# Turning convolved rows on VectorE instead of TensorE in a window-attention and depthwise-convolution kernel

## The chip, the cores and the metric

The kernel runs on one core of a Trainium2 chip. The core has five engines with queues of their own: TensorE (PE in the profile, its weight loads PEld), VectorE (DVE), ScalarE (ACT), GpSimd (POOL) and SyncE (SP), and 16 DMA engines that move data. The metric is device time in microseconds (us); less is better.

## The reference

Sixteen images of 56 x 56 positions with 384 channels, all float32, go through two layers, each added to its input:

```
x = x + window_attention(group_norm(x))     # shifted by 3, windows 7 x 7, 12 heads of 32
x = x + depthwise_conv3x3(group_norm(x))    # one 3x3 filter per channel, clipped to -1..1, then its sign
```

The group norm has 32 groups of 12 channels and no weights of its own. The second one needs the whole image of the first layer's result before its mean and variance are known, so the convolution of an image can start only when its attention is over.

## The kernel before

*Strips and units.* An image is 8 strips of 7 rows, one row of windows each. A strip (392 positions) is held channels by positions, in 3 chunks of 128 channels. Half a strip, 4 windows, is a unit: 256 units in all, 16 an image. `all_units` walks them. In each unit the heavy work is written in 6 steps (`heavy`): queries, keys (`query_key`, L464) and values (`value`, L477) of the next strip, the scores of the next unit (`scores`, L518), this unit's sums over the exponentials (`add_up`, L589), weighting (`attend`, L609) and, in second halves, the projection (`project`, L648). Around them DVE adds the bias (`softmax`, L535), ACT takes the exponential (`exponential`, L553) and the inverse of the sums (`invert`, L627 and L628, then L629 and L630 on DVE). There is one score buffer in PSUM, which the scores of the next unit may overwrite only after L629 has read the sums.

*Values by key.* `turn` transposes values in squares of 32 on DVE (L488), and `by_key` moves them to their places by 16 DMAs a strip on SP's queue, in pieces of 128 bytes (L500). Input strips are read by POOL's queue in 128-byte pieces (L411) and turned by DVE in squares of 32 (`turn_halves`, L428).

*Light work.* Functions with a time in units are put into a list by `at(when, f, ...)`; in each unit, after each of the 6 steps, those whose time has come are written out in order of time. The order of the program on each engine and on each queue is thus set by these times; an engine and a queue work strictly in that order.

*Convolution.* `project` writes the first layer's result, channels by positions, to DRAM (`mids`). `plan_conv` works on the previous image beside the attention of the current one. The image is cut into 4 bands of BR = 14 rows, times 3 chunks. For each band and chunk, every 1.3 units (0.95 for image 14): `band` loads 14 rows and their neighbours on SP's queue (L696); `pad` writes the normalised rows into a padded buffer (ACT, L711; one border row cleared by POOL where the band is at an edge); `middle` starts the sum with the centre tap and the residual (ACT, L723); eight `tap`s add the other taps on DVE (L736), each a multiply-add over 128 x 784 elements that reads and writes the same sum. When the 3 chunks of a band are done, `store` turns the sums on PE (L747: seven tiles of 112 positions, 3 transposes each, into one PSUM bank), ACT copies the bank out (L748), and SP's queue writes rows of 1,536 bytes, two tiles a DMA (L752).

*The last image* has nothing to hide behind. `plan_last` lays it out after the last unit: `norm_late` (the norm by matmuls, without DRAM), then per band chunks 0 and 1 as above on DVE, and chunk 2 on PE (`convolve`, L773 and L780: the taps as matmuls with diagonal weights, which also turn the sums; `carry` copies and stores, L788 and L791). The bands are loaded one after the other into two buffers of `bpool`. At the very end a check that numbers stayed in range decides on a slower second pass (not taken here).

Of the kernel before, what the change touches and what calls it, by code (L numbers as in the profile page):

```python
# [15 lines left out]
WIN = 7  # L16
# [18 lines left out]
def kernel(  # L35
# [27 lines left out]
    BR = 14  # L63
    NB = H // BR
    R = W + SHIFT
# [6 lines left out]
    LG = 2  # L72
# [9 lines left out]
    io = ctx.enter_context(tc.tile_pool(name="io", bufs=3))  # L82
# [3 lines left out]
    bpool = ctx.enter_context(tc.tile_pool(name="xb", bufs=2))  # L86
    opool = ctx.enter_context(tc.tile_pool(name="o", bufs=5))
# [37 lines left out]

    spare = [
# [11 lines left out]
    def clear_more():  # L138
        nc.gpsimd.memset(power, -0.5)
        nc.gpsimd.memset(ones, 1.0)  # L140
        nc.gpsimd.memset(least, LEAST)
        nc.gpsimd.memset(seen, 0.0)
        for t in (qk[:, :, ST:], *hps):
            nc.gpsimd.memset(t, 0.0)

    def clear_again():
        for t in spare:
            nc.vector.memset(t, 0.0)
# [22 lines left out]
    def load_depthwise():  # L171
        wl = [io.tile([P, LG, C], F32, tag="io", name=f"dwl{n}")[:9, 0, :] for n in range(3)]
        nc.scalar.dma_start(wl[0], w_dw.rearrange("a b c o -> (a b) (c o)"))
        for c in range(NC):
            nc.scalar.dma_start(bo_sb[:, c : c + 1], b_out[c * P : (c + 1) * P].unsqueeze(1))

        nc.vector.tensor_scalar(wl[1], wl[0], -1.0, 1.0, ALU.max, ALU.min)
        nc.vector.tensor_scalar(wl[0], wl[1], 0.0, None, ALU.is_gt)
        nc.vector.tensor_scalar(wl[2], wl[1], 0.0, None, ALU.is_lt)
        nc.vector.tensor_tensor(wl[0], wl[0], wl[2], ALU.subtract)  # L180
        nc.vector.tensor_tensor(wl[0], wl[0], wl[1], ALU.subtract)
        nc.vector.tensor_tensor(wl[0], wl[0], wl[1], ALU.add)  # L182
        pw = bank("pdw")
        for c in range(NC):
            nc.tensor.transpose(pw[:, c * 9 : (c + 1) * 9], wl[0][:, c * P : (c + 1) * P], ident[:9, :9])
        nc.vector.tensor_copy(dw_t, pw[:, : NC * 9].rearrange("p (c t) -> p c t", c=NC))
# [106 lines left out]
    def fetch_late():  # L293

        pairs = group_blocks(C, GS)
        gm = xpool.tile([P, NC, ST], F32, tag="x", name="gm").rearrange("p c n -> p (c n)")[:, : len(pairs) * P]
        gm = gm.rearrange("p (n q) -> p n q", q=P)
        nc.sync.dma_start(gm, gmat)
        dg = xpool.tile([P, NC, ST], F32, tag="x", name="dg").rearrange("p c n -> p (c n)")[:, : 9 * P]
        dg = dg.rearrange("p (t q) -> p t q", q=P)  # L300
        hp = xpool.tile([P, NC, ST], F32, tag="x", name="hp_late").rearrange("p c n -> p (c n)")
        hp = hp[:, : (BR + 2) * (W + 2)].rearrange("p (h w) -> p h w", w=W + 2)
        acc = xpool.tile([P, NC, ST], F32, tag="x", name="acc_late").rearrange("p c n -> p (c n)")
        acc = acc[:, : BR * (W + 2)].rearrange("p (h w) -> p h w", w=W + 2)
        for t in (hp, acc):
            nc.gpsimd.memset(t, 0.0)
        late_tiles.update(gm=gm, dg=dg, hp=hp, acc=acc)
# [382 lines left out]
    def band(b, k, c):  # L690

        lo, hi = max(k * BR - 1, 0), min((k + 1) * BR + 1, H)
        at = lo - (k * BR - 1)
        xb = bpool.tile([P, BR + 2, R], F32, tag="xb", name=f"xb_{b}_{k}_{c}")
        rows = xb[:, at : at + hi - lo, :]
        nc.sync.dma_start(rows, mids[b][:, c, lo:hi, :])  # L696
        bands[b, k, c] = (xb, rows, at, hi - lo)
# [3 lines left out]
    def pad(b, k, c, late=False):  # L701

        coef, cen = coefs[1, b], centers[b]
        xb, rows, at, n = bands.pop((b, k, c))
        hp = late_tiles["hp"] if late else hps[count[0] % 2]
        count[0] += not late
        if k == 0:
            nc.gpsimd.memset(hp[:, 0, :], 0.0)
        if k == NB - 1:
            nc.gpsimd.memset(hp[:, BR + 1, :], 0.0)  # L710
        nc.scalar.activation(  # L711
            hp[:, at : at + n, 1 : W + 1],
            rows[:, :, 0:W],
            AF.Identity,
            bias=coef[:, c, 1:2],
            scale=coef[:, c, 0:1],
        )
        padded[b, k, c] = (hp, xb)

    def middle(b, k, c, late=False):  # L720
        hp, xb = padded[b, k, c]
        acc = late_tiles["acc"] if late else opool.tile([P, BR, W], F32, tag="o", name=f"o_{b}_{k}_{c}")
        nc.scalar.activation(  # L723
            acc[:, :, :W],
            xb[:, 1 : BR + 1, 0:W],
            AF.Identity,
            bias=centers[b][:, c, 1:2],
            scale=centers[b][:, c, 0:1],
        )
        outs[b, k, c] = acc  # L730

    def tap(b, k, c, t):
        dy, dx = divmod(t, 3)
        acc = outs[b, k, c]
        hp, _ = padded[b, k, c]
        nc.vector.scalar_tensor_tensor(  # L736
            acc, hp[:, dy : dy + BR, dx : dx + W], dw_t[:, c, t : t + 1], acc, ALU.mult, ALU.add
        )

    def store(b, k, g, chunks=NC):  # L740
        todo = range(g * LG, min((g + 1) * LG, BR * W // OT))
        flat = [outs[b, k, c].rearrange("p h w -> p (h w)") for c in range(chunks)]
        xo = io.tile([P, LG, C], F32, tag="io", name=f"xo_{b}_{k}_{g}")
        for n, t in enumerate(todo):
            po = bank(f"px_{b}_{k}_{t}")
            for c in range(chunks):
                nc.tensor.transpose(po[:OT, c * P : (c + 1) * P], flat[c][:, t * OT : (t + 1) * OT], ident)  # L747
            nc.scalar.copy(xo[:OT, n, : chunks * P], po[:OT, : chunks * P])  # L748
        n = len(todo)
        first = k * BR * W + g * LG * OT  # L750
        rows = out[b].rearrange("h w c -> (h w) c")[first : first + n * OT, : chunks * P]
        nc.sync.dma_start(rows.rearrange("(t p) c -> p t c", p=OT), xo[:OT, :n, : chunks * P])  # L752
# [3 lines left out]
    def convolve(b, k, c):  # L756
# [5 lines left out]
        tiles = BR * W // OT  # L762
# [19 lines left out]
    def carry(b, k, c):  # L782

        by_token = xpool.tile([P, NC, ST], F32, tag="x", name=f"xc_{k}").rearrange("p c n -> p (c n)")
        tiles = BR * W // OT
# [3 lines left out]
        rows = out[b].rearrange("h w c -> (h w) c")[k * BR * W : (k + 1) * BR * W, c * P : (c + 1) * P]  # L789
# [5 lines left out]

    def plan_last(b, first):

        at(first, norm_late, b)
        at(first + 0.1, center, b, nc.vector)
        for k in range(NB):  # L800
            for c in (2, 0, 1):
                n = 2 * k + c
                when = first + 0.5 + (2 * k if c == 2 else n)
                at(when - (0.1 if c == 2 else 0.2), band, b, k, c)
                at(when - (0.05 if c == 2 else 0.15), pad, b, k, c, c == 2)
                at(when - (0.04 if c == 2 else 0.14), middle, b, k, c, c == 2)
                if c == 2:
                    at(when + 0.2, convolve, b, k, c)
                    at(when + 1.3, carry, b, k, c)
                    continue  # L810
                for i, t in enumerate((0, 1, 2, 3, 5, 6, 7, 8)):
                    at(when + i / 8, tap, b, k, c, t)
            for g in range(-(-BR * W // OT // LG)):
                at(first + 0.5 + 2 * k + 2.02 + 0.01 * g, store, b, k, g, NC - 1)
# [7 lines left out]
    def plan_conv(p, first, step, lead, late, queue):  # L822
# [5 lines left out]
        for n in range(NB * NC):  # L828
            k, c = divmod(n, NC)
            when = first + step * n  # L830
            at(when - 1.3 * step, band, p, k, c)
            at(when - 0.65 * step, pad, p, k, c)
            at(when - 0.45 * step, middle, p, k, c)
            for i, t in enumerate((0, 1, 2, 3, 5, 6, 7, 8)):
                at(when + step * i / 8, tap, p, k, c, t)
            if c == NC - 1:
                tiles = -(-BR * W // OT // LG)
                for g in range(tiles):
                    at(when + step + late + 0.3 * g, store, p, k, g)
# [18 lines left out]
    def heavy(u):  # L858
# [13 lines left out]
        if more:  # L872
            todo[1 if half else 2 * NC - 1].append((by_key, (s + 1, half)))
# [8 lines left out]
    def plan(last_queue):  # L882
        for b in range(1, B):
            plan_load(b)
            plan_conv(b - 1, NU * b, 1.3 if b < B - 1 else 0.95, 3, 0.6, nc.gpsimd)
        at(B * NU - 6, fetch_late)
        for t in range(9):
            at(B * NU - 5 + 0.3 * t, diagonal, t)

    def all_units(fast):  # L890
# [42 lines left out]
        plan_last(B - 1, B * NU)  # L933
# [112 lines left out]
```

## Time and profile before

| | |
|---|---|
| device time, median of 3 runs | 4287.52 us (4286.94 to 4291.69) |
| device time of the profiled execution | 4289.45 us |
| its span | 4287.3 us |
| granted TensorE clock, mean over the span | 0.989 |
| DMA engines, mean share busy, 1000 to 1250 us | 0.49 |
| first and last exponential (L553) | 83.9 and 4148.4 us |
| last projection on PE (L648) | 4161.2 us |
| first tap of the last image | 4174.1 us |

The span starts at the first instruction of the profiled execution. "Busy" is the time in which an engine had an instruction running; for PE it is pipelined, so a busy PE need not be at its peak. In a line of a group, the numbers after the bar are busy time in all and the mean duration of one instruction in ns, then the idle time of the engine just before these instructions and what ended it. In a line of a stretch the figures are PE, PEld, DVE, ACT and POOL busy (with the number of instructions), the granted clock, the DMA engines' share and GB/s. In a line of order in time they are start, duration, engine, line, operation, output <- inputs. In a line of a DMA queue they are packets, MB, and the share of 16 engines' time in that stretch.

### The profile page before, as it was taken

How to read it: one execution, taken by the hardware profiler on the slowest of the kernel's cores; microseconds unless marked ns; L12 is line 12 of the kernel's file. 1: busy time of each engine (PE TensorE's matmuls, PEld its weight loads, DVE VectorE, ACT ScalarE, POOL GpSimd, SP SyncE). 2: the span in 40 equal slices, each digit the busy share in tenths (PEclk: the TensorE clock that was granted, in tenths of full speed). 3: DMA queues.
4: the chain of work that ended last, by engine and by line, in shares of the span. 5: the costliest groups of instructions: out<-in, count | busy, mean ns of one | idle time of the engine just before them, and what ended most of it. 6: DMA issues, size and time to landing. Idle time of an engine off the chain costs nothing. (4 is left out here: it accounts for less than half of the span.)

```text
span 4287.3 us, 156586 instructions
## 1 busy us (share of the span) xinstructions
PE 4182.8 (98%) x68545; PEld 2688.1 (63%) x68545; DVE 3448.4 (80%) x4367; ACT 2482.8 (58%) x5286; POOL 1796.1 (42%) x3160
## 2 busy tenths in 40 slices
PE   5999999999999999999999999999999999999986
PEld 3666666666666666666666666666666666666656
DVE  4556888788887888878888897888889788887875
ACT  2545656566565656656565665656656565665542
POOL 4453545354443544535345443535445344451000
PEclk8999999999999999999999999999999999999988
DMA  4434445454444545445454444545544454543432
GB/s 90 80 66 82 105 106 123 103 109 108 110 100 106 120 99 116 107 100 121 96 114 111 107 103 106 117 106 110 109 107 105 105 122 99 114 105 80 105 97 86
DMA packets 1000294, 445.33 MB, mean 104 GB/s; under 512 B 876922, under 2 KB 938203, under 8 KB 999602
## 3 DMA queue, kind: packets, MB, share of 16 engines
q1 hardware_dynamic: 909776, 273.72, 30.7%
q0 software_dynamic: 87648, 159.12, 15.3%
q8 instruction: 542, 8.88, 0.9%
q10 hardware_dynamic: 2178, 2.38, 0.2%
q14 instruction: 150, 1.23, 0.1%
HBM read 175.31 MB, written 158.46 MB: 78 GB/s over the span
## 5 line engine op out<-in xcount | busy, mean ns | idle before, releaser
L464 PE MATMUL pq<-xn,wq_t 128*128 128x392 f32 x4608 | 1590.5, 496 | 0.4 <-ACT ot L619 0.2
L736 DVE SCALAR_TENSOR_TENSOR o<-hp,dw_t,o 128x784 f32<-128x784 f32 x1504 | 1527.5, 1020 | 49.1 <-ACT o L723 35.8
L411 POOL DMA_DIRECT2D xl<-in_x_dram x1980 | 1328.7, 725 | 179.6 <-DVE xt L428 105.4
L464 PEld LDWEIGHTS pq<-xn,wq_t 128*128 128x128 f32 x4608 | 844.1, 188 | 587.0 <-issue 1.6
L648 PE MATMUL py<-ot,wo_t 128*128 128x392 f32 x2304 | 817.9, 497 | 1.6 <-DVE ot L637 1.6
L477 PE MATMUL pv<-xn,wq_t 128*128 128x392 f32 x2304 | 817.9, 496 | 1.2 <-ACT xn L453 1.2
L471 ACT COPY qk<-pq 128x392 f32<-128x392 f32 x768 | 371.4, 484 | 700.8 <-PE pq L464 697.4
L629 DVE SCALAR_TENSOR_TENSOR ln<-ps,inv 128x588 f32<-128x588 f32 x256 | 197.1, 770 | 538.2 <-ACT inv L628 538.2
L668 POOL COPY y<-y 128x63 f32<-128x63 f32 x128 | 34.1, 267 | 1389.1 <-DVE y L656 1389.0
L477 PEld LDWEIGHTS pv<-xn,wq_t 128*128 128x128 f32 x2304 | 420.8, 189 | 284.9 <-ACT xn L453 2.4
L648 PEld LDWEIGHTS py<-ot,wo_t 128*128 128x128 f32 x2304 | 420.6, 190 | 271.8 <-DVE ot L637 1.9
L484 ACT COPY vt<-pv 128x392 f32<-128x392 f32 x384 | 189.1, 493 | 449.1 <-PE pv L477 448.1
L553 ACT ACTIVATE e<-e 128x1176 f32<-128x1176 f32 x256 | 303.1, 1184 | 236.3 <-DVE e L535 236.3
L518 PEld LDWEIGHTS ps<-qk 32*64 32x64 f32 x24576 | 309.4, 131 | 146.6 <-issue 109.2
L609 PE MATMUL po<-e,v 49*32 49x49 f32 x24576 | 364.0, 212 | 8.1 <-DMA v<-vq 7.8
L535 DVE SCALAR_TENSOR_TENSOR e<-ps,bias 128x1176 f32<-128x1176 f32 x256 | 349.2, 1364 | 25.9 <-PE ps L518 24.7
L609 PEld LDWEIGHTS po<-e,v 49*32 49x32 f32 x24576 | 354.6, 105 | 14.2 <-issue 8.3
L518 PE MATMUL ps<-qk 32*64 32x49 f32 x24576 | 342.1, 226 | 3.5 <-DVE ln L629 2.6
L440 ACT COPY x<-xt 128x196 f32<-128x196 f32 x720 | 225.8, 369 | 93.4 <-DVE xt L428 92.2
L488 DVE STREAM_TRANSPOSE vq<-vt 128x512 f32<-128x512 f32 x384 | 267.6, 698 | 6.7 <-ACT vt L484 6.5
L656 DVE TENSOR_TENSOR y<-py,x 128x392 f32<-128x392 f32 x384 | 215.1, 560 | 62.7 <-PE py L648 57.5
L453 ACT ACTIVATE xn<-x,coef 128x392 f32<-128x392 f32 x384 | 247.2, 713 | 13.9 <-DVE dwl L182 13.9
(152 smaller groups left out, 3722.8 us busy)
## 6 DMA issues: line engine op xcount, KB each, us to landing
v<-vq SPq DMA_DIRECT2D x2048, 48.0 KB
mid<-y POOLq DMA_DIRECT2D x112, 619.5 KB
xl<-in_x_dram POOLq DMA_DIRECT2D x1260, 52.5 KB
out_dram<-xo SPq DMA_DIRECT2D x180, 336.0 KB
xb<-mid SPq DMA_DIRECT2D x96, 472.0 KB
xb<-mid SPq DMA_DIRECT2D x96, 442.5 KB
out_dram<-xo SPq DMA_DIRECT2D x60, 168.0 KB
mid<-y POOLq DMA_DIRECT2D x15, 354.0 KB
```

The costliest lines, as they stand in the source:

```text
L411: nc.gpsimd.dma_start(xz[i * D + lo : i * D + hi, c, k : k + n, :], flat[token : token + n * (hi - lo)].rearrange("(k t) c -> t k c", k=n) ...
L453: nc.scalar.activation(xn[:, c, :, :T], xs[s][:, c, :].rearrange("p (w t) -> p w t", t=T), AF.Identity, bias=coef[:, c, 1:2], scale=coef[: ...
L464: nc.tensor.matmul(pq[:, :ST].rearrange("p (w t) -> p w t", t=T), wq_t[:, c, m * P : (m + 1) * P], xn[:, c, :, :T], start=(c == 0), stop=( ...
L471: nc.scalar.copy(qk[:, m, :ST], pq[:, :ST])
L477: nc.tensor.matmul(pv[:, :ST].rearrange("p (w t) -> p w t", t=T), wq_t[:, c, 2 * C + m * P : 2 * C + (m + 1) * P], xn[:, c, :, :T], start= ...
L488: nc.vector.transpose(vq[:, :, :, m].rearrange("p h n d -> p n h d"), vt[:, m].rearrange("p (n w) (j b) -> p n (w j) b", w=2, b=D),)
L518: nc.tensor.matmul(pp[row * HT : (row + 1) * HT, i, k0 : k0 + T], qk[part, NC * fast + j, q0 : q0 + HT], qk[part, NC * (not fast) + j, q0 ...
L535: nc.vector.scalar_tensor_tensor(e, pp[:, :, : NC * 2 * T].rearrange("q i (n k) -> q i n k", k=T), QSCALE, bias[:, int(s % NS == NS - 1)]. ...
L553: nc.scalar.activation(flat, flat, AF.Exp, accum_out=reach[:, 0, u : u + 1])
L609: nc.tensor.matmul(po[w][i * D : (i + 1) * D, (2 * j + r) * T : (2 * j + r + 1) * T], vs[s][keys, n * 2 + r, h * D : (h + 1) * D], by_head ...
L648: nc.tensor.matmul(py[:, :ST], wo_t[:, c, m * P : (m + 1) * P], ots[s][:, c, :], start=(c == 0), stop=(c == NC - 1),)
L736: nc.vector.scalar_tensor_tensor(acc, hp[:, dy : dy + BR, dx : dx + W], dw_t[:, c, t : t + 1], acc, ALU.mult, ALU.add)
```

## The change

Bands become 28 rows (2 an image), with LR = 14 kept for what PE convolves in the last image. The sum of a band and chunk lies in one of two fixed buffers `accs`, each row of 56 as two halves of 28 in fields of 32 elements. After the eight taps, `turn_sum` transposes this buffer in place on DVE in squares of 32, so that 28 of each 32 partitions hold positions and the free dimension holds 32 channels. `store` then writes from it directly, in eight DMAs per band and chunk (2 halves x 4 groups of 32 channels), each of 28 x 28 pieces of 32 channels, 128 bytes. The PE transposes, the copies by ACT and the buffers `io` and `opool` go; `bpool` has one buffer in place of two.

A band and chunk takes 2.6 units (1.95 for image 14) in place of 1.3 (0.95). `by_key` is written wholly into the first half of a strip, after steps 3 and 5, where before its second part came after step 1 of the second half.

For the last image all bands but one are loaded ahead: from 1.2 units before the end the rows that the last strip does not touch, and the remaining rows when the strip is stored; they lie in `xpool` tiles and in the `qk` and `bias` tiles, which nothing reads any more by then. The centre tap of the first chunk is started by DVE, that of the first PE chunk by POOL. Band 0 leaves by `turn_sum` and `store`; band 1 is turned by PE (`turn_late`: 14 transposes of 128 x 128 for each chunk, copies by ACT, and stores in pieces of 512 bytes).

```diff
-    BR = 14
+    BR = 28
     NB = H // BR
+    LR = BR // 2
...
-    bpool = ctx.enter_context(tc.tile_pool(name="xb", bufs=2))
-    opool = ctx.enter_context(tc.tile_pool(name="o", bufs=5))
+    bpool = ctx.enter_context(tc.tile_pool(name="xb", bufs=1))
...
+    accs = [const.tile([P, 2 * BR, D], F32, tag=f"o{n}", name=f"o{n}") for n in range(2)]
...
-        for t in (qk[:, :, ST:], *hps):
+        for t in (qk[:, :, ST:], *hps, *accs):
             nc.gpsimd.memset(t, 0.0)
...
+    def band_late(b, k, c, part):
+        rows = LR if c == NC - 1 else BR
+        lo, hi = max(k * rows - 1, 0), min((k + 1) * rows + 1, H)
+        first = k * rows - 1
...
+        parts = [(last_strip[0][1], last_strip[1][0])] if part == 0 else last_strip
+        for p0, p1 in parts:
+            p0, p1 = max(p0, lo), min(p1, hi)
+            if p0 < p1:
+                nc.sync.dma_start(xb[:, p0 - first : p1 - first, :], mids[b][:, c, p0:p1, :])
...
+    def by_half(t):
+        return t.rearrange("p h (a w) -> p h a w", a=2)
+
+    def sum_of(b, k, c):
+        return outs[b, k, c].rearrange("p (h a) w -> p h a w", a=2)[:, :, :, :HR]
...
         nc.vector.scalar_tensor_tensor(
-            acc, hp[:, dy : dy + BR, dx : dx + W], dw_t[:, c, t : t + 1], acc, ALU.mult, ALU.add
+            acc, by_half(hp[:, dy : dy + BR, dx : dx + W]), dw_t[:, c, t : t + 1], acc, ALU.mult, ALU.add
         )
...
-    def store(b, k, g, chunks=NC):
-        todo = range(g * LG, min((g + 1) * LG, BR * W // OT))
...
-                nc.tensor.transpose(po[:OT, c * P : (c + 1) * P], flat[c][:, t * OT : (t + 1) * OT], ident)
-            nc.scalar.copy(xo[:OT, n, : chunks * P], po[:OT, : chunks * P])
...
-        nc.sync.dma_start(rows.rearrange("(t p) c -> p t c", p=OT), xo[:OT, :n, : chunks * P])
+    def turn_sum(b, k, c):
+        flat = outs[b, k, c].rearrange("p h w -> p (h w)")
+        nc.vector.transpose(flat, flat)
+
+    def store(b, k, c, part):
+        half, i = divmod(part, HPC)
+        first = (k * BR + half * BR // 2) * W
+        rows = out[b].rearrange("h w c -> (h w) c")[first : first + BR // 2 * W]
+        nc.sync.dma_start(
+            rows.rearrange("(h t) c -> t h c", t=HR)[:, :, c * P + i * D : c * P + (i + 1) * D],
+            outs[b, k, c][i * D : i * D + HR, half * BR : (half + 1) * BR, :],
+        )
...
+    def turn_late(b, k, c, half, end):
+        flat = outs[b, k, c].rearrange("p h w -> p (h w)")
+        tiles = BR // 4
...
+                nc.tensor.transpose(po[:, i * P : (i + 1) * P], flat[:, t * P : (t + 1) * P], ident)
+            copy = nc.vector.tensor_copy if end and first else nc.scalar.copy
+            copy(xo[:, first * P : (first + n) * P], po[:, : n * P])
...
+        for j in range(4):
+            queue = nc.scalar if end and j % 2 else nc.sync
+            queue.dma_start(rows[j], xo[j * D : j * D + HR, : tiles * P].rearrange("p (t c) -> p t c", c=P))
...
     def plan_conv(p, first, step, lead, late, queue):
...
-            at(when - 1.3 * step, band, p, k, c)
-            at(when - 0.65 * step, pad, p, k, c)
-            at(when - 0.45 * step, middle, p, k, c)
+            at(when - 0.75 * step, band, p, k, c)
+            at(when - 0.35 * step, pad, p, k, c)
+            at(when - 0.25 * step, middle, p, k, c)
             for i, t in enumerate((0, 1, 2, 3, 5, 6, 7, 8)):
-                at(when + step * i / 8, tap, p, k, c, t)
-            if c == NC - 1:
-                tiles = -(-BR * W // OT // LG)
-                for g in range(tiles):
-                    at(when + step + late + 0.3 * g, store, p, k, g)
+                at(when + step * i / 9, tap, p, k, c, t)
+            at(when + step * 8 / 9, turn_sum, p, k, c)
+            for part in range(2 * HPC):
+                at(when + step * 8 / 9 + late + 0.1 * part, store, p, k, c, part)
...
-        if more:
-            todo[1 if half else 2 * NC - 1].append((by_key, (s + 1, half)))
+        if more and not half:
+            for part in range(2):
+                todo[NC + 2 * part].append((by_key, (s + 1, part)))
...
-            plan_conv(b - 1, NU * b, 1.3 if b < B - 1 else 0.95, 3, 0.6, nc.gpsimd)
+            plan_conv(b - 1, NU * b, 2.6 if b < B - 1 else 1.95, 3, 0.4, nc.gpsimd)
```

The tail's plan, with the four DVE chunks in a row and one PE chunk beside each:

```diff
+        chunks = [(k, c) for k in range(NB) for c in range(NC - 1)]
+        bands_late = [(0, NC - 1), chunks[0], (1, NC - 1), chunks[1], (2, NC - 1), chunks[2], (3, NC - 1)]
+        for n, (k, c) in enumerate(bands_late):
+            at(first - 1.2 + 0.1 * n, band_late, b, k, c, 0)
+            at(first - 0.04 + 0.001 * n, band_late, b, k, c, 1)
...
+        for n, (k, c) in enumerate(chunks):
+            when = first + 1 + n
+            if n == len(chunks) - 1:
+                for part in range(2):
+                    at(when - 1.9, band_late, b, k, c, part)
...
+            for i, t in enumerate((0, 1, 2, 3, 5, 6, 7, 8)):
+                at(when + i / 8, tap, b, k, c, t)
+            if k == 0:
+                at(when + 0.99, turn_sum, b, k, c)
+                for part in range(2 * HPC):
+                    at(when + 1.01 + 0.05 * part, store, b, k, c, part)
+            else:
+                for half in range(2):
+                    at(when + 1.15 + 0.01 * half, turn_late, b, k, c, half, n == len(chunks) - 1)
+            k, c = n, NC - 1
...
+            at(when + 0.1, convolve, b, k, c)
+            at(when + 1.1, carry, b, k, c)
```

## The prediction, made before the changed kernel was run

> **What bounds the kernel now.** I read the page's busy times and slices first, then the starts of the exponential (L553, one per unit of half a strip), then stretches, groups, waits, and the tail.
>
> ```profile
> span 4287.3 us, 156586 instructions
> PE 4182.8 (98%) x68545; PEld 2688.1 (63%) x68545; DVE 3448.4 (80%) x4367; ACT 2482.8 (58%) x5286; POOL 1796.1 (42%) x3160
> ...
> PE   5999999999999999999999999999999999999986
> ```
>
> PE is full in all but the first and the last two slices. Busy PE alone proves little, so I look for a stretch of the same work without the transposes that the change removes. Image 0 is one: no convolution runs beside it.
>
> ```profile
> 123.19 1.18 ACT L553 ACTIVATE e<-e 128x1176 f32<-128x1176 f32 x1 [1.28 <-DVE e L535]
> ...
> 369.76 1.18 ACT L553 ACTIVATE e<-e 128x1176 f32<-128x1176 f32 x1 [1.32 <-DVE e L535]
> ...
> 284.80:315.60 30.80, 30.80 (x521) 19.27 (x521) 12.66 (x18) 12.98 (x27) 11.38 (x18) 1.00 0.38 78
> 2000.00:2250.00 250.00, 250.00 (x4195) 158.95 (x4192) 210.84 (x264) 150.94 (x321) 116.55 (x203) 1.00 0.50 109
> ```
>
> The two starts are 16 units apart: 15.41 us a unit. From 369.76 to the last start, 4148.4, are 237 units: 15.94 us each. PE (first busy figure) is full in both stretches at a granted clock of 1.00, so the 0.53 us between them is PE work. DVE (third) is 41% busy in the first and 84% in the second, and PE does not care. So PE bounds the main loop, DVE is next. The tail after the last projection (4162 to 4287.3) is different: there eight chains of eight taps (L736) follow one another on DVE.
>
> **The change, part by part.**
>
> *Transposes leave PE.* Groups and PE's order:
>
> ```profile
> L747 PE MATMUL px<-ident,o 128*112 128x128 f32 x1316 | 192.4, 279 | 33.0 <-ACT xo L748 26.8 <-DVE o L736 6.2
> ...
> 2058.37 0.82 PE L747 MATMUL px<-ident,o 128*112 128x128 f32 x6
> 2059.03 2.14 PE L648 MATMUL py<-ot,wo_t 128*128 128x392 f32 x6
> ```
>
> 1260 of the 1316 belong to images 0 to 14 (15 x 4 bands x 7 tiles x 3 chunks). Six delay the next matmul by 0.66 us, 110 ns each: 139 us. The other way, 237 units x 0.53 us, gives 126. I take **-130 us**. The 420 copies xo (L748, 183 us) leave ACT, which at 58% is not the bound: nothing by itself.
>
> *DVE gets the turning, and fewer, longer taps.*
>
> ```profile
> L736 DVE SCALAR_TENSOR_TENSOR o<-hp,dw_t,o 128x784 f32<-128x784 f32 x1504 | 1527.5, 1020 | 49.1 <-ACT o L723 35.8
> L428 DVE STREAM_TRANSPOSE xt<-xl 128x1440 f32<-128x1440 f32 x120 | 200.4, 1670 | 0.0
> L488 DVE STREAM_TRANSPOSE vq<-vt 128x512 f32<-128x512 f32 x384 | 267.6, 698 | 6.7 <-ACT vt L484 6.5
> L656 DVE TENSOR_TENSOR y<-py,x 128x392 f32<-128x392 f32 x384 | 215.1, 560 | 62.7 <-PE py L648 57.5
> ...
> DVE ln L629 <- ACT inv L628: 538.2, 236, 8.4
> ```
>
> The transposes L428 and L488 differ by 928 elements and 972 ns: 1.05 ns an element. One of 1792 elements takes 1670 + 352 x 1.05 = 2.04 us; 90 of them 184 us (at L488's 1.36 ns an element 2.44 us and 220). A tap starts 0.95 us after the one before it (1.02 long, ends overlap); 784 elements more at 1.04 ns (the slope of the rows for 588 and 1176 elements, 770 and 1364 ns, is 1.01) give 1.77. So 1440 x 0.95 = 1368 us become 720 x 1.77 = 1274: -94. Rows cut to 28 elements cost nothing by L656, which walks rows of 7 and takes 560 ns for 392. Net +90 us, 0.35 a unit: DVE goes from 13.45 (210.84/250 of 15.94) to 13.8 us, in a unit of 15.4. It fits, at 90%. What hides it is DVE's wait for the chain add-up, logarithm, inverse: in 1000 to 2000 us it is 120.7 us in 62.7 units, 1.9 a unit. It would shrink by 0.35 + 0.53 to about 1.0. Without that cover PE waits: a late L535 or L629 delays the sums (L589) or the scores (L518). Behind each 2 us transpose stand the next softmax and inverse. Scores ended at 2024.9 and their sums began at 2031.0; the softmax addition and exponential need 2.8 us of it, so some 3 us of lateness go unseen. Bounds: 0, or 0.88 x 237 = 209 if the wait were rigid; 20 of 256 inverses already found DVE late while PE stayed full, which is nearer the first. I take **+17 us**.
>
> *ACT and POOL.* Pads and middles halve in number and double in size (784 elements 1046 ns, 896 1135: 0.8 ns an element, so 1568 take some 1.7 us): ACT gains time, but each blocks 0.6 us longer. A single band buffer makes the load wait for the previous middle: it is issued half a step (20 us) after that, 16 us before its pad. More memsets at the start (some 5 us on POOL by L144) end before POOL's wait of 6.67 us for xl at 38.6: 0.
>
> *Stores in pieces of 128 bytes.* Eight stores per chunk of a band replace the seven wide ones per band; each has 28 x 28 = 784 pieces, 6,272 a step of 2.6 units, on SP's queue, which also carries the v loads and bands. The trace has no such store. Nearest rows:
>
> ```profile
> q1 hardware_dynamic: 6136, 0.76, 27.1%
> ...
> q1 hardware_dynamic: 798, 0.46, 75.9%
> ```
>
> The first is 316 to 335 us, v pieces of 128 bytes within SBUF: 27.1% of 16 x 19 us over 6136 is 13.4 ns a piece. The second is 4192.9 to 4195.2, nearly all 512-byte pieces of out_dram<-xc: 35 ns. So 5.3 to 13.7 us a step over 16 engines; I take 20 ns, 7.8 us. The engines are busy 0.50 of a step of 41.5 us now, 20.8 us, of which the wide stores (0.8 MB at the tail's 264 GB/s) are 3: the sum is 23 to 32 of 40 us. No stall: 0. On SP's queue a v issue (384 pieces) takes 0.62 us, so a store about 1.1; with 21 v issues a step that is 22 of 40 us. A v load queued behind stores has slack: PE waited 7.8 us for v in the whole run, and part 1 of each load is now issued at 5/6 of the first half-strip, no longer in the second.
>
> Against this stands the Trainium skill, "DMA: Bandwidth & Descriptors", Specifications: below 512 bytes a DMA engine does a read-modify-write. If that doubled the 512-byte row, a step's stores would take 27 us and the engines would be full, as in the last rival below. The same page ("Why a DMA increments its semaphore by 16 and not by 1") says that 28 partitions spread over 14 engines only; no row here shows it, and it would make the 7.8 us 8.9.
>
> *The tail.*
>
> ```profile
> 4174.12 8.53 DVE L736 SCALAR_TENSOR_TENSOR o<-hp,dw_t,o 128x784 f32<-128x784 f32 x8 [1.75 <-ACT o L723]
> ...
> 4199.71 8.53 DVE L736 SCALAR_TENSOR_TENSOR o<-hp,dw_t,o 128x784 f32<-128x784 f32 x8 [8.62 <-ACT o L723]
> ...
> 4267.86 8.60 DVE L736 SCALAR_TENSOR_TENSOR o<-hp,dw_t,o 128x784 f32<-128x784 f32 x8 [3.06 <-ACT o L723]
> ```
>
> From 4174.1 to 4276.5 run 64 dependent taps at 1.07 us, 68 us; the other 34 are waits for bands (xb<-mid). After: 32 taps at 1.07 + 0.82 = 1.88, 60 us, two turns 4, and bands that already lie there. Chunk 3 writes the buffer of chunk 1, whose eight stores (1.1 to 1.9 us each) and a band lie before it: a gap of 0 to 15, taken as 5. So 69 against 102.4 us; the end after the last tap (10.8 us) keeps its shape: **-34 us** (-20 to -45).
>
> Sum on the span: 4287.3 - 130 + 17 - 34 = **4140 us**. The profiled execution took 4289.45 and the median of the runs is 4287.52, so span and median agree within 0.3 us.
>
> **Rivals.**
> 1. *DVE becomes the bound.* For it: 90% busy, in order, instructions twice as long. Against: it is 84% busy now and PE never shows it. If the 1.9 us wait a unit stays, a unit is 13.8 + 1.9 = 15.7: 237 x 0.24 = 57 us gained in place of 113: about 4195.
> 2. *The transposes were hidden.* If PE's real limit were elsewhere, only the tail gains: 4253. Against: 15.41 beside 15.94 at the same clock, both full.
> 3. *Slower: the stores fill the DMA engines.* 6,272 pieces a step take 57 ns each before 17.8 + stores pass 40 us, and from some 60 ns a step is longer than its 41.5. At twice the 512-byte row, 70 ns: 45.2 us, 90 x 3.7 = 333 us more, less 34: about 4585. Against: 13 to 35 ns in the rows; for: no store of that size was seen.
>
> **How the numbers follow.** Forecast 0.66 (own range 4105 to 4178: DVE loss 0 to 45, tail -45 to -20); rival 1 0.18 (4178 to 4235); rival 2 0.06 (4235 to 4290, a third of it within 0.2%); rival 3 0.10. The range 4103 to 4228 leaves out rival 3, rival 2 and the edges. About 0.2% (9 us) separates a change from none: faster 0.88, same 0.02, slower 0.10.
>
> **What would show it.** Exponential starts 15.4 to 15.5 us apart in images 1 to 15; a 128x1792 transpose near 2.0 us and a 1568-element tap near 1.8; the inverse's wait down to about half; DMA share 0.55 to 0.7 with PE waiting for v no more than some 10 us; taps in the tail nearly back to back. It is wrong if the starts lie 15.7 or more apart with PE waiting for L629 or L535 (rival 1), or if waits for v, bands or buffers appear on PE, ACT or DVE with the DMA share near 1 (rival 3).

## The result, and the profile after

| | before | changed | ratio, 95% interval |
|---|---|---|---|
| median of 4 runs each, us | 4288.54 | 4212.02 | 0.9821 [0.9804, 0.9838] |
| lowest to highest, us | 4286.94 to 4291.69 | 4207.24 to 4217.27 | |
| span of the profiled execution, us | 4287.3 | 4211.4 | |

The change is faster by 76 us (1.8%). The forecast was 148 us: the time lies inside the predicted range of 4103 to 4228, but above the part of it that the forecast had for itself (4105 to 4178) and in the part given to rival 1 (4178 to 4235). Half of the gain is missing, and the rest of this document looks for it. First the head of the changed kernel's page: the span, busy times of each engine, and PE in 40 slices.

```profile
span 4211.4 us, 153120 instructions
...
PE 4068.7 (97%) x67257; PEld 2565.1 (61%) x67257; DVE 3495.2 (83%) x3711; ACT 2232.3 (53%) x4654; POOL 1863.9 (44%) x3165
...
PE   5999999999999999999999999999999999999997
```

PE's busy time has fallen by 114 us (4182.8 before), and still every slice but the first and the last shows a 9. The tenths are too coarse for what follows; two stretches of 250 us show it. The columns are busy time (and count) of PE, PEld, DVE, ACT and POOL, then granted clock, DMA share, GB/s.

```profile
1000.00:1250.00 250.00, 244.71 (x4061) 152.09 (x4059) 216.29 (x227) 138.11 (x291) 120.23 (x201) 1.00 0.57 108
2000.00:2250.00 250.00, 245.14 (x4140) 152.86 (x4124) 217.29 (x227) 136.91 (x286) 118.88 (x200) 1.00 0.58 109
```

Before, PE had 250.00 of 250 here; now it idles for 5 of 250 us. Over 3700 us of such work that is about 75 us: PE no longer bounds every unit. Where it idles is seen from the starts of the exponential, one per unit (L561 is now its line), and from what stands around one of them. The timeline's columns are start, duration, engine, line, operation, tiles and count; in brackets the idle time before, and what ended it.

```profile
370.36 1.19 ACT L561 ACTIVATE e<-e 128x1176 f32<-128x1176 f32 x1 [1.40 <-DVE e L543]
...
1994.84 1.19 ACT L561 ACTIVATE e<-e 128x1176 f32<-128x1176 f32 x1 [0.71 <-DVE e L543]
1998.81 6.44 SPq L508 DMA_DIRECT2D v<-vq  x8
2005.29 2.76 SPq L798 DMA_DIRECT2D out_dram<-o  x4
2008.10 6.32 SPq L508 DMA_DIRECT2D v<-vq  x8
2010.95 1.19 ACT L561 ACTIVATE e<-e 128x1176 f32<-128x1176 f32 x1 [3.29 <-DVE e L543]
2014.59 0.48 SPq L703 DMA_DIRECT2D xb<-mid  x1
2019.82 1.75 ACT L748 ACTIVATE hp<-xb,coef 128x1624 f32<-128x1624 f32 x1 [7.59 <-DMA xb<-mid]
2021.47 0.47 ACT L492 COPY vt<-pv 128x392 f32<-128x392 f32 x1
2021.99 2.24 PE L485 MATMUL pv<-xn,wq_t 128*128 128x392 f32 x6 [2.62 <-ACT vt L492]
2023.44 0.77 DVE L637 SCALAR_TENSOR_TENSOR ln<-ps,inv 128x588 f32<-128x588 f32 x1 [6.86 <-ACT inv L636]
2032.19 1.19 ACT L561 ACTIVATE e<-e 128x1176 f32<-128x1176 f32 x1 [2.27 <-DVE e L543]
...
4102.00 1.18 ACT L561 ACTIVATE e<-e 128x1176 f32<-128x1176 f32 x1 [7.68 <-DVE e L543]
```

From 370.36 to 4102.00 are 237 units: 15.745 us each (15.944 before; 15.4 to 15.5 forecast). The mean hides that one unit in each of images 1 to 14 takes 20 to 22 us, here 2010.95 to 2032.19, and the others 12.6 to 18.3 (12.8 to 19.4 before). In it SP's queue issues 8 v loads, 4 stores and 8 v loads in a row from 1998.81, and only then, at 2014.59, the next band. The band lands 5.2 us later. ACT has stood at the pad L748 for 7.59 us by then, and had reached it 2.4 us before the band was even issued. Behind the pad on ACT's queue are a vt copy and the logarithm and inverse: PE waits for the copy, which frees its PSUM tile (2.62 us), and DVE for the inverse (6.86 us). The waits of 350 to 4080 us (total, times, longest), the first line from the kernel before, show what is new: ACT's wait for the band, which the kernel before does not have. DVE's wait for the inverse was there already.

```profile
DVE ln L629 <- ACT inv L628: 455.6, 215, 8.4
...
DVE ln L637 <- ACT inv L636: 391.7, 162, 8.4
...
ACT hp L748 <- DMA xb<-mid: 104.0, 16, 8.6
```

In the groups (busy, mean ns of one, then idle before) the prices that the prediction estimated are now measured:

```profile
L784 DVE SCALAR_TENSOR_TENSOR o<-hp,dw_t,o 128x1568 f32<-128x1568 f32 x752 | 1378.5, 1833 | 5.4
L791 DVE STREAM_TRANSPOSE o<-o 128x1792 f32<-128x1792 f32 x92 | 186.0, 2022 | 0.1
L748 ACT ACTIVATE hp<-xb,coef 128x1624 f32<-128x1624 f32 x90 | 158.0, 1756 | 104.0 <-DMA xb<-mid 104.0
L778 ACT ACTIVATE o<-xb,cen 128x1568 f32<-128x1568 f32 x91 | 155.2, 1706 | 13.2 <-DMA out_dram<-o 10.8 <-issue 2.0
```

A stretch in which SP's queue carries stores and hardly anything else, 2110 to 2125 us, gives the price of a store's piece (packets, MB, share of 16 engines):

```profile
q1 hardware_dynamic: 3192, 0.40, 19.0%
```

19.0% of 16 x 15 us over 3192 packets is 14.3 ns each: a 128-byte piece to HBM costs the DMA engine about what the 13.4 ns pieces of v within SBUF did. The Trainium skill, "DMA: Bandwidth & Descriptors", Specifications, says that a transfer below 512 bytes makes the engine read, modify and write; whatever it does here, a piece costs less than half of the 35 ns of the 512-byte pieces before, though 1.6 times as much a byte.

The tail, last image:

```profile
4128.48 1.86 DVE L776 TENSOR_SCALAR o<-xb,cen 128x1568 f32<-128x1568 f32 x1 [0.17 <-DVE cen L695]
4130.49 15.06 DVE L784 SCALAR_TENSOR_TENSOR o<-hp,dw_t,o 128x1568 f32<-128x1568 f32 x8
...
4164.58 30.14 DVE L784 SCALAR_TENSOR_TENSOR o<-hp,dw_t,o 128x1568 f32<-128x1568 f32 x16
...
4189.50 1.91 PE L822 MATMUL pc<-xl,hp_late 128*114 128x128 f32 x16
...
4191.46 0.93 PE L855 MATMUL px<-ident,o 128*128 128x128 f32 x7
4192.10 0.97 ACT L857 COPY xo<-px 128x512 f32<-128x512 f32 x2 [12.76 <-PE px L855]
...
4193.09 6.23 SPq L863 DMA_DIRECT2D out_dram<-xo  x8
4199.42 1.03 SPq L840 DMA_DIRECT2D out_dram<-vq  x2
4200.55 4.02 SPq L863 DMA_DIRECT2D out_dram<-xo  x4
```

The taps run without a gap from 4130.49 to 4194.7, 64.2 us where there were 102.4. From the last exponential to the first tap it is 28.5 us (25.7 before), and from the last tap to the end 16.7 (10.8 before). In these 16.7 us and just before lie 14 issues of SP's queue from 4193.09 on, 8 of them for a chunk whose taps had ended near 4179.6 but whose transposes (px, L855) stood on PE behind a convolution until 4191.46.

### The profile page after: what moved, and what is told of

It is laid out like the page before. It is cut to its first block, busy times and chain, and to the rows that moved or that the text cites. A ratio compares the mean times of both kernels' runs of the same rounds, so it can differ in the third digit from the quotient of the medians.

```text
span 4211.4 us, 153120 instructions
## 1 busy us (share of the span) xinstructions
PE 4068.7 (97%) x67257; PEld 2565.1 (61%) x67257; DVE 3495.2 (83%) x3711; ACT 2232.3 (53%) x4654; POOL 1863.9 (44%) x3165
## 4 chain that ended last, share of the span: by engine, by line
PE 40%; issue 16%; DVE 14%; POOL 12%; DMA 10%; SPq 4%; ACT 3%; DVEq 0%; ACTq 0%; POOLq 0%
PE pq L472 16%; POOL xl L419 9%; PE pv L485 8%; PE py L656 8%; DVE o L784 6%; PE ps L526 3%; SPq L508 3%; PE po L617 3%; DMA xl<-in_x_dram 3%; DMA mid<-y 2%; PE ps L597 2%; DMA xb<-mid 2%; DVE e L543 1%; SPq L798 1%; DVE xt L436 1%
## 5 line engine op out<-in xcount | busy, mean ns | idle before, releaser
L784 DVE SCALAR_TENSOR_TENSOR o<-hp,dw_t,o 128x1568 f32<-128x1568 f32 x752 | 1378.5, 1833 | 5.4
L485 PE MATMUL pv<-xn,wq_t 128*128 128x392 f32 x2304 | 827.3, 502 | 35.5 <-ACT vt L492 30.6
L676 POOL COPY y<-y 128x63 f32<-128x63 f32 x128 | 46.3, 362 | 1299.0 <-DVE y L664 1299.0
L637 DVE SCALAR_TENSOR_TENSOR ln<-ps,inv 128x588 f32<-128x588 f32 x256 | 195.3, 763 | 467.7 <-ACT inv L636 467.6
L561 ACT ACTIVATE e<-e 128x1176 f32<-128x1176 f32 x256 | 303.4, 1185 | 456.1 <-DVE e L543 454.2
L617 PE MATMUL po<-e,v 49*32 49x49 f32 x24576 | 374.1, 212 | 12.3 <-DMA v<-vq 10.7
```

The costliest lines, as they stand in the source:

```text
L485: nc.tensor.matmul(pv[:, :ST].rearrange("p (w t) -> p w t", t=T), wq_t[:, c, 2 * C + m * P : 2 * C + (m + 1) * P], xn[:, c, :, :T], start= ...
L561: nc.scalar.activation(flat, flat, AF.Exp, accum_out=reach[:, 0, u : u + 1])
L617: nc.tensor.matmul(po[w][i * D : (i + 1) * D, (2 * j + r) * T : (2 * j + r + 1) * T], vs[s][keys, n * 2 + r, h * D : (h + 1) * D], by_head ...
L784: nc.vector.scalar_tensor_tensor(acc, by_half(hp[:, dy : dy + BR, dx : dx + W]), dw_t[:, c, t : t + 1], acc, ALU.mult, ALU.add)
```

## The experiments

Theory A: the missing gain is the late band. The changed plan issues all 16 v loads of a strip in one unit, with stores between, and the band's place in the plan falls behind them on SP's queue. Rivals: rival 1 of the prediction (DVE has become the bound), rival 2 (the transposes were hidden) and rival 3 (the stores crowd the DMA engines). Runs with the same letter in the table ran on one chip, beside the same runs of the kernel before, and differences of a few us are taken only between these. The changed kernel ran where the kernel before took 4288.54, within 0.7 us of chips a and b, so its 4212.02 is compared with both, for differences of tens of us.

| run | chip | before, us | this, us | ratio, 95% interval | us a unit, images 1 to 15 |
|---|---|---|---|---|---|
| e1_band_early | a | 4287.9 | 4152.36 | 0.9682 [0.9666, 0.9698] | 15.488 |
| e2_by_key_split | a | 4287.9 | 4157.03 | 0.9699 [0.9683, 0.9716] | 15.490 |
| e3_turn_one_square | a | 4287.9 | 4193.26 | 0.9782 [0.9765, 0.9798] | 15.641 |
| e4_before_no_store | a | 4287.9 | 4157.92 | 0.9695 [0.9679, 0.9711] | 15.386 |
| e5_band_act_queue | b | 4288.1 | 4157.23 | 0.9701 [0.9685, 0.9717] | 15.513 |
| e6_early_one_square | b | 4288.1 | 4144.01 | 0.9663 [0.9647, 0.9679] | 15.459 |
| e7_early_no_store | b | 4288.1 | 4141.65 | 0.9661 [0.9645, 0.9677] | 15.444 |
| e8_early_tail | b | 4288.1 | 4149.80 | 0.9683 [0.9667, 0.9700] | 15.482 |
| e9_tail_and_split | c | 4285.31 | 4155.89 | 0.9699 [0.9685, 0.9712] | 15.514 |
| e8_again | c | 4285.31 | 4143.29 | 0.9668 [0.9655, 0.9681] | 15.459 |
| e1_again | c | 4285.31 | 4143.70 | 0.9672 [0.9659, 0.9686] | 15.461 |

The last column is the time from the start of the 19th exponential to the last one over 237 units, in the profiled execution.

**1. The band a fifth of a step earlier, for images 0 to 13** (image 14 has the shorter step).

```diff
-            at(when - 0.75 * step, band, p, k, c)
+            at(when - (0.95 if step > 2 else 0.75) * step, band, p, k, c)
```

> The changed kernel with one time altered: in images 0 to 14 but the last of them a band is asked for 0.95 of a step before its taps, no longer 0.75. Theory A (the band of the fourth chunk of each image stands on SP's queue behind 16 v loads and 4 stores, lands late, and its pad holds ACT and then PE): the one unit per image of 20 to 21 us falls to 15 to 16, ACT's wait for xb<-mid falls from 104 us to under 25, and the time falls by 60 to 85 us, to 4125 to 4150. Theory B (DVE, at 87 to 90% busy, is what holds the units back): the long unit is a backlog of DVE, and the time falls by less than 20 us, to 4195 or more. Theory C (the DMA engines, 57% busy, deliver late whatever the order): less than 20 us as well, with the wait moved to another chunk.

Measured 4152.36 us, 60 below the changed kernel and 2 above theory A's range. The same place of the program in its timeline:

```profile
1957.14 0.36 SPq L703 DMA_DIRECT2D xb<-mid  x1
...
1967.19 5.94 SPq L508 DMA_DIRECT2D v<-vq  x8
1973.18 2.77 SPq L798 DMA_DIRECT2D out_dram<-o  x4
1975.99 6.30 SPq L508 DMA_DIRECT2D v<-vq  x8
1979.32 1.18 ACT L561 ACTIVATE e<-e 128x1176 f32<-128x1176 f32 x1 [3.05 <-DVE e L543]
1980.50 1.74 ACT L748 ACTIVATE hp<-xb,coef 128x1624 f32<-128x1624 f32 x1
...
1995.02 1.18 ACT L561 ACTIVATE e<-e 128x1176 f32<-128x1176 f32 x1 [1.56 <-DVE e L543]
```

The v loads and stores stand in the same run of 15 us, but the band leaves before them; the pad follows the exponential at once, and the unit takes 15.7 us in place of 21.2. The wait for the band is gone from its list of waits. PE is back at 248.6 of 250, and DVE, with the same work, is at 220 to 222 of 250 in place of 216 to 217: it was not the bound in the changed kernel, it waited too.

```profile
2000.00:2250.00 250.00, 248.58 (x4196) 155.08 (x4184) 220.04 (x233) 140.01 (x293) 121.98 (x204) 0.99 0.59 110
```

**2. The v loads back in two units, the band left where the change has it.**

```diff
-        if more and not half:
-            for part in range(2):
-                todo[NC + 2 * part].append((by_key, (s + 1, part)))
+        if more:
+            todo[1 if half else 2 * NC - 1].append((by_key, (s + 1, half)))
```

> The changed kernel with the v loads of a strip written where they were before the change: 8 after step 6 of the first half-strip, 8 after step 2 of the second. Theory A: the late band stands behind 8 v loads in place of 16, some 6 us sooner, of the 7.6 us that its pad waits: the long unit falls to 15 to 17 us and the time to 4130 to 4165, unless the later v loads make PE wait (over 10 us in all of waits for v). Theory B and C: within 15 us of the changed kernel.

Measured 4157.03, 55 below the changed kernel, with no wait for a band. So the late band needs both: its own place in the plan, and the 16 v loads gathered ahead of it.

**3. The band on ACT's queue at the same place of the plan.**

```diff
-        nc.sync.dma_start(xb[:, at : at + hi - lo, :], mids[b][:, c, lo:hi, :])
+        nc.scalar.dma_start(xb[:, at : at + hi - lo, :], mids[b][:, c, lo:hi, :])
```

> The changed kernel with one edit: the band load of the loop (L703) is issued from ScalarE's queue in place of SyncE's, at the same place of the plan. Question: was the band late because its issue stood behind two v loads and the stores on SyncE's queue (theory A), or because the DMA engines, or the single band buffer, give it late whatever queue it is issued from (rival)? In the changed kernel the late band was issued at 2014.59 us behind v loads of 6.44 and 6.32 us and stores of 2.76 us, and landed 5.2 us later. Theory A: issued on ScalarE it leaves up to 15 us earlier, the wait of L748 for the band is gone from the list of waits, no exponential of an image is 20 us after the one before, and the time is that of the runs with an early band, 4152 and 4157, give or take 8 for the issue's own time on ScalarE: 4145 to 4165. Rival: the wait stays at about 100 us in 16, the time within 15 us of 4212.

Measured 4157.23. The same place:

```profile
1973.33 6.28 SPq L508 DMA_DIRECT2D v<-vq  x8
1973.78 0.33 ACTq L703 DMA_DIRECT2D xb<-mid  x1
...
1986.94 1.74 ACT L748 ACTIVATE hp<-xb,coef 128x1624 f32<-128x1624 f32 x1
```

The band is issued beside the first v loads, not 15.8 us after the first of them, and the pad has no idle time before it. The DMA engines' share (last figure but one) is shown for the time in which the band stood on SP's queue in the changed kernel, for its transfer there, and for its transfer here:

```profile
1998.80:2014.60 15.80, 15.80 (x266) 9.51 (x264) 15.05 (x17) 8.53 (x22) 15.66 (x28) 1.00 0.64 96
2014.60:2019.80 5.20, 4.47 (x135) 3.07 (x134) 1.98 (x2) 0.00 (x0) 2.98 (x4) 1.00 0.95 238
...
1973.80:1979.00 5.20, 5.20 (x140) 3.55 (x140) 4.56 (x6) 4.54 (x14) 4.82 (x9) 1.00 0.97 235
```

The engines were not full while the band waited to be issued, and as busy during its transfer in one run as in the other. Neither the single band buffer nor the DMA engines made it late; the order on SP's queue did. It does so to more bands than the one that shows. From a band's issue to its pad, which the plan puts 16 us apart, the six loads of image 1 have 5.5, 11.0, 21.4, 4.9, 7.7 and 22.6 us in the changed kernel (issues from 625.21 us on) and 16.7, 22.0, 15.6, 13.2, 15.6 and 16.3 from ACT's queue (from 607.34 on). Four of six have lost 8 to 11 us of lead; only the fourth is left with so little that ACT stands. The Trainium skill, "DMA: Bandwidth & Descriptors", Rules for kernel authors, says that spreading transfers over the issuing engines doesn't help bandwidth and only saves the sequencer's issue time; bandwidth is indeed not what changed here (DMA share 0.59 and 0.60 in the two stretches of 250 us, 0.57 and 0.58 in the changed kernel), but issue time on the right load was worth 55 us. That settles theory A: three edits that share nothing but this order each bring back 55 to 60 us.

**4. Only one square of each chunk turned, the band still late.** Images 0 to 14 leave all columns but the first 32 of each chunk's rows unturned.

```diff
-        nc.vector.transpose(flat, flat)
+        n = flat.shape[1] if b == B - 1 else D
+        nc.vector.transpose(flat[:, :n], flat[:, :n])
```

> The changed kernel with only the first 32 of the 1792 columns of each sum turned in images 0 to 14 (the rest of those sums is stored unturned, so that part of the computation is left out): DVE loses some 1.8 us in each of 90 chunks, 165 us in all, and all else stays. Theory B: the time falls by 50 us or more. Theory A: the long unit per image stays near 20 us, and the time falls by less than 25 us.

Measured 4193.26: taking almost all of the turning off DVE brings 19 us, a third of what one moved load brings, and the long unit stays (18.2 to 19.7 us), as does the wait for the band in 350 to 4080 us:

```profile
ACT hp L748 <- DMA xb<-mid: 62.9, 13, 6.0
```

It was 104.0 with all columns turned, so the turning has a share in how late the band is, but a small one in the time. Rival 1 falls.

**5. The kernel before without its transposes, copies and stores for images 0 to 14** (these images are not written).

```diff
-            if c == NC - 1:
-                tiles = -(-BR * W // OT // LG)
-                for g in range(tiles):
-                    at(when + step + late + 0.3 * g, store, p, k, g)
```

> The kernel before with the transposes, copies and stores of the convolved rows left out in images 0 to 14 (those images are not written). If the transposes cost PE 110 ns each on the path, units of images 1 to 15 are 15.4 us apart in place of 15.94 and the time falls by 120 to 140 us, to 4150 to 4170. If they were hidden, it falls by less than 30 us.

Measured 4157.92: 4287.90 - 4157.92 = 130.0 us. ACT's copies and the wide stores are left out with the transposes, but PE is full in both kernels, so the time is PE's:

```profile
2000.00:2250.00 250.00, 250.00 (x4175) 155.82 (x4173) 219.24 (x278) 144.64 (x306) 116.94 (x206) 1.00 0.46 93
```

Rival 2 (hidden transposes) is refuted. The budget on chip a is now 4287.9 - 130.0 - 29.5 (the tail, from the two traces) = 4128.4. The early band reaches 4152.4, so 24 us are left; the loops agree: (15.488 - 15.386) x 237 = 24.2 us. Part of it belongs to the chip: on chip c the early band takes 4143.70 (e1_again), 8.7 less than on chip a, while the kernel before takes 2.6 less, so there the same budget leaves 17.9. Three runs look into the 24.

**6. Early band, one square turned** (edits 1 and 4 together).

> The run with the early band (4152.4 us) with one more edit: in images 0 to 14 only the first 32 columns of a chunk's rows are turned (the other columns of these images leave unturned, so this part of the computation is left out); image 15 whole. It takes 8 x 15 turns of some 2.02 us down to one square. Question: what are the 24 us by which the early band stays above 4128.4 (4287.9 less 130.0 of the transposes, less 29.5 of the tail)? Theory: the prediction's VectorE term (17 us taken, bounds 0 and 209): the turns make VectorE's part of the recurrence late, so without most of them the time falls by 12 to 24, to 4128 to 4140. Rival: the 24 us come from the transfers or from SyncE's queue, which this edit leaves as they are: within 6 us of 4152.

**7. Early band, no stores for images 0 to 14** (these images are not written).

```diff
-            for part in range(2 * HPC):
-                at(when + step * 8 / 9 + late + 0.1 * part, store, p, k, c, part)
```

> The run with the early band (4152.4 us) without the stores of images 0 to 14 (these images are not written, which leaves that part of the computation out). Question: do the pieces of 128 bytes cost anything once no band waits behind their issues? By the changed kernel's rows a piece takes 14.3 ns of a DMA engine and a store 0.58 us of SyncE's queue, so the prediction's price of nothing for the stores stands: the time falls by 6 us at most, to 4146 to 4153. Rival (the stores crowd the v loads or the queue): it falls by 15 us or more, below 4138, and PE's wait for v falls from its 10.7 us.

These two ran on chip b, where the early band's loop (in e8_early_tail, which differs from run 1 in the tail alone) takes 15.482 us a unit. One square: 15.459, so (15.482 - 15.459) x 237 = 5.4 us for the 90 turns (the expectation's "8 x 15" miscounts them). No stores: 15.444, so 9.0 us. Both expectations were missed, each between its two cases: the turns cost less than 12, the stores more than 6 but no 15. PE's matmuls wait 4.8 us for v in 350 to 4080 us of e8_early_tail, and its weight loads, which overlap them, 4.8; neither waits in run 7, so at least that wait comes with the stores. If the two simply add, some 8 of the 24 us stay unexplained; longer taps and pads, which hold DVE and ACT for twice as long each, were not tried alone.

**8. The early band, and in the tail px of the chunk next to last ahead of the fourth and last convolution.**

```diff
-                    at(when + 1.15 + 0.01 * half, turn_late, b, k, c, half, n == len(chunks) - 1)
+                    at(when + (1.15 if n == len(chunks) - 1 else 1.05) + 0.01 * half, turn_late, b, k, c, half, n == len(chunks) - 1)
```

> The run with the early band (4152.4 us) with the last image's store of its chunk next to last put into the plan 0.10 of a unit earlier, ahead of the third convolution of PE. In the changed kernel that chunk's taps had ended at about 4179.6 us and its px of PE came at 4191.46, behind the convolution, so that 18 stores were issued in a row from 4193.1 to 4204.6 and the end came 16.7 us after the last tap. Theory: the chunk's stores now leave during VectorE's last taps, the end falls to 11 to 13 us after the last tap, and the time to 4146 to 4149. Rival: the px waits on PE for its taps and holds up the convolution behind it, so that the gain is given back: 4150 to 4160.

> The early band with the earlier store in the tail, a second time, beside the early band alone on the same chip. Theory: the tail is worth the 3.4 us by which the spans differ (4150.0 and 4146.6), so the two times stand 2 to 5 us apart. Rival: it is worth nothing, within 1 us.

> The early band alone, a second time, for the comparison of the tail on the same chip. Theory: 4149 to 4155 us, 2 to 5 above the run with the earlier store in the tail. Rival: within 1 us of it.

On chip b the time, 4149.80, lies between the two cases. On chip c the two medians stand 0.4 us apart (4143.29 and 4143.70), as the rival has it, and the spans of one execution each 2.7 (4141.1 and 4143.8), as the theory has it. The mechanism works as far as the stores go, and part of it is given back, as the trace of e8_again shows:

```profile
4110.58 0.93 PE L855 MATMUL px<-ident,o 128*128 128x128 f32 x7
...
4112.21 4.88 SPq L863 DMA_DIRECT2D out_dram<-xo  x8
...
4125.07 1.91 PE L822 MATMUL pc<-xl,hp_late 128*114 128x128 f32 x16
...
4127.03 1.69 PE L855 MATMUL px<-ident,o 128*128 128x128 f32 x14
```

The 8 stores leave while the last taps run, but now the convolution ends later: the last px waits for it until 4127.03, 2.6 us after the last tap (4124.45). From the last tap to the end it is 16.7 us, where 11 to 13 were expected, and 19.0 in e1_again (4143.8 - 4124.85). What this edit is worth in time is not settled; it is too small for these runs.

**9. All of it, with the v loads in two units.** Edits 1, 2 and 8: part 0 of the v loads goes at the end of a strip's first half, part 1 early in its second (the expectation has the halves the wrong way round).

> The run with the early band and the earlier store of the tail (4149.8 us) with the v loads put back where the kernel before has them: part 0 late in the second half-strip's unit before, part 1 in the next, in place of both in one unit. Question: do the 10.7 us that went with the stores of images 0 to 14 (4152.4 to 4141.7) come from v loads that stand behind stores on SyncE's queue, so that spreading them helps? Theory: yes, in part; PE's wait for v falls and the time goes to 4138 to 4146. Rival: with bands early, the place of the v loads is worth nothing more: 4146 to 4153.

Measured 4155.89, 12.6 slower than e8_again on the same chip: neither case. Once the band is early, gathering the v loads, as the change does, is the better place; spread, the wait of PE's matmuls for v in 350 to 4080 us rises from 1.7 to 6.8 us, which is part of it. Where the rest goes is open. The best version is the change with the early band: 4143.70 us on chip c, 0.9672 [0.9659, 0.9686] of the kernel before, and 4152.36 on chip a, against 4212.02 for the change as given.

## Why the prediction was half right

The time lies in the stated range by luck: the forecast's own mechanism stops at 4178, and what brought the time to 4212 is a wait that neither the forecast nor a rival priced.

- **Transposes leave PE, -130.** Right in mechanism and size: run 5 measured 130.0. PE full beside the same work without them was enough evidence.
- **DVE, +17.** The prices held: a turn 2.022 us (2.04 forecast), a tap 1.833 (1.02 + 0.82 = 1.84 of length forecast). With the band early (e8_early_tail) DVE is busy 221.6 of 250 us in a unit of 15.48, 13.7 us (13.8 forecast), and PE nearly full. The turns themselves cost 5.4 us (run 6). DVE's cover shrank less than forecast: its wait for the inverse was to fall to about half, and fell in 350 to 4080 us from 455.6 to 391.7, and to 322.5 with the early band. Rival 1's mark, units of 15.7 or more, did appear, at 15.745, but with another cause: in the long unit DVE itself waited 6.86 us at L637 (once L629) for ACT, which the pad blocked.
- **ACT and POOL, 0: this is the step that failed.** "it is issued half a step (20 us) after that, 16 us before its pad" took the place in the plan for the time of the issue. 16 us is also what stood ahead of it on SP's queue: 8 v loads, 4 stores and 8 v loads, 15.5 us. The step's price was about +60 us (4212.0 - 4152.4; by the loops (15.745 - 15.488) x 237 = 61).
- **Stores, 0.** A piece took 14.3 ns (20 assumed), a store 0.58 us of SP's queue (1.1 assumed, by the number of pieces), and the DMA share was 0.57 over 250 us: rival 3 had no ground. The term is 9 us by run 7, not 0. But the queue was checked for its mean only ("22 of 40 us"), and for the v loads' slack, not for the band's. The sentence that part 1 of the v loads "is now issued at 5/6 of the first half-strip" held the cause; it was not asked what stands behind them on the queue.
- **Tail, -34.** Measured -29.5: the spans differ by 75.9 and the last exponentials by 46.4 (4148.4 and 4102.0). Taps -38.2 (-33.4 forecast: no gap came), the start +2.8 (0 forecast; 2.4 of it has gathered when the norm's last step, L695, once L687, ends, before the first middle, and its cause is open), the end +5.9 (0 forecast; PE's and SP's order is in the lines above, but run 8 does not settle how much of it that is).

Sum on chip a: -130 + 24 (for DVE's 17 and the stores' 0) + 60 (for 0) - 29.5 (for -34) = -75.5, beside -76 measured. The 24 and the 60 are themselves differences of these times, so the sum has to close; what stands behind them are the units, 24.2 and 61 us. The marks for rival 3 asked for waits for bands with the DMA share near 1; the band was held back while it was 0.64, which neither the forecast nor a rival described.

## What to carry to other kernels

A load that the plan puts 16 us ahead is that early only if nothing long stands before it on its queue: for each moved load, list what the same queue issues between its due time and the wait for it, in one run and not as a mean over the step. When a change gathers transfers on a queue, the victim is the next single load behind them, and the engine that shows the stall (here DVE, waiting for ACT) may be two steps from the queue. One long unit in sixteen hides in a mean; print the distances between starts.

## What the runs showed of the hardware

- A store of 784 pieces of 128 bytes took 0.58 us on SP's queue (median of 704, 0.32 to 3.16), a v load of 384 pieces 0.62 (median of 1895, 0.59 to 2.89), and 0.8 in a run of eight (6.44 us): between these two the issue's time does not follow the number of pieces.
- A 128-byte piece from SBUF to HBM took 14.3 ns of a DMA engine, and the 512-byte pieces of the tail before 35.
- The band's issue took 0.33 us on ACT's queue and 0.50 on SP's (medians of 90; 0.33 to 0.36 and 0.35 to 2.41): what made it late was the 15.8 us ahead of it, not its own issue.
